# Turning the normed rows of 13 feed-forward blocks with VectorE's 32 x 32 squares and two DMAs, one round ahead, instead of with TensorE's transposes

## The chip, the core and the metric

The kernel runs on one core of a Trainium2 chip. The metric is the device time of one execution in microseconds (us). TensorE (PE) multiplies matrices and writes to PSUM; VectorE (DVE), ScalarE (ACT) and GpSimd (POOL) work element by element; SyncE (SP) only issues DMAs here. PEld is TensorE's weight load. Each engine takes its own instructions strictly in order and waits, where it must, on semaphores of the others.

## What is computed

`x` has 2 x 2048 rows of 256 numbers in float32. Four layers are added to it in turn, each working on layer-normed rows (mean taken off, divided by the standard deviation):

```python
x = x + attn_a(layernorm(x))   # gated scan along the rows of a sequence
x = x + ffn(layernorm(x))      # first feed-forward layer
x = x + attn_b(layernorm(x))   # linear attention, 16 heads, recurrent over the rows
x = x + ffn(layernorm(x))      # second feed-forward layer, same weights
# ffn(y) = gelu(y @ ternary(W1).T + b1) @ ternary(W2).T + b2,  256 -> 1024 -> 256
# ternary(W): each weight is rounded to -1, 0 or 1 by the mean size of W
```

TensorE sums over the partition axis, so the normed rows, which lie with rows on partitions, must be turned (features on partitions) before `y @ W1`. This turning is what the change touches.

## The kernel before

The 4096 rows lie in SBUF as `x_sb`, 32 chunks of 128 rows. Four chunks make a block of 512 rows, so there are 8 blocks (`blocks`, the two sequences in turn). The order of PE, DVE, ACT and POOL instructions is written out by hand (`manual_schedule`); only SP's DMAs are put in order by the framework.

**One feed-forward round** takes one block. `ffn_in` (L491) has 8 steps, one for each 128 hidden features: four matmuls of 512 columns into one PSUM bank (L498; the rows come as two parts, `xh`, the value rounded to fp32r, and `xl`, the rest), then ACT's gelu (L504); after each second step `Hidden.split` calls `halves` (L201): ACT rounds 1024 numbers to `hh` (L203) and DVE subtracts to get `hl` (L204). `ffn_out` (L509) has 8 steps of 8 matmuls (L520); step f needs `hh` and `hl` number f // 2. At its end DVE adds the result to `x_sb` (L529) and, in the second layer, SP stores it (L531).

**Turning.** `norm_stats` (L156) takes four pairs of DVE instructions (L163, L164) and then a chain of small POOL instructions that makes scale and bias of the rows, `rs` and `nb`: L175 (add), L176 (power), L180, L181. `norm_rows` (L184) writes the normed rows `xn` with four ACT instructions (L195). `turned_halves` (L209) turns them: 8 TensorE transposes of 128 x 128 (L216) into two PSUM banks `pt`, and for each bank `halves`: ACT writes `xh` from PSUM (L203), DVE writes `xl` (L204). `ffn_bias` (L534) adds b2 to the next block's rows of `x_sb` with one long POOL instruction (L537). The next round's first matmuls need `xh` and `xl`.

**Another way to turn is already in the kernel.** `norm_squares` (L277): DVE transposes every 32 x 32 square of the rows (L260, `sq`), SP writes them to DRAM (L263, `dsqxn`), SP reads them back with four DMAs that put the squares in their places (L271, `rawxn`, which must wait for the first DMA to land), and `halves_end` (L302) makes `xh` and `xl` out of that in one ACT and one DVE instruction that read with a stride. The attention turns its own rows so, and so is block 1 of the second layer turned (`second_squares`, `second_turned`).

**The front** (L546) holds the scan layer and the first feed-forward layer. After a prologue it runs 8 rounds, i = 0 to 7. Rounds 0 to 3 also carry a unit of the scan: its matmuls (L389, by `scan_steps`) stand between the first four steps of `ffn_in`, and its way back into rows (`a_`, transposes L426, DVE adds L428) and, in rounds 0 to 2, the turning of the next unit's rows (`t_`, TensorE transposes L240, ACT L244 with gamma) stand between steps of `ffn_out`. In rounds 0 to 3 the stats of block i + 2 are taken after `ffn_out` (`fs_`) and the rows of block i + 1 between steps of `ffn_in` (`fr_`). Rounds 4 to 6 also hold `weights_kv` (L463), four POOL instructions of 128 x 512 each. In round 0 to 6, `ft_(i + 1)` turns the next block in the midst of `ffn_out`.

**The attention** follows (not touched), and then the second feed-forward layer, the loop at L1270, called ffn2 below: 8 rounds, of which the first only ends block 0 (its steps, `last.outs`, began within the attention), and rounds 1 to 6 turn block i + 1 on TensorE.

The PSUM banks are given out in rings: six banks ("ps") for everything but the results of `ffn_out`, which have two ("out"). A bank is used again when the ring comes round to it, so TensorE waits if its reader is late.

Of the kernel before, what the change touches and what calls it, by code (L numbers as in the profile page):

```python
# [44 lines left out]
def kernel(  # L45
# [272 lines left out]
    def ternary_sum(pool, w, name, on_vector):  # L318
        wf = w.rearrange("p c e -> p (c e)")
        n = wf.shape[1] // D  # L320
        part = pool.tile([P, n], FP, tag="part", name=f"part_{name}")
        if on_vector:
            nc.vector.tensor_reduce(
                part, wf.rearrange("p (a e) -> p a e", e=D), AX.X, ALU.add, apply_absolute_value=True
            )
            return part
        for k in range(n):
            size = pool.tile([P, D], FP, tag="abs", name=f"abs_{name}{k}")
            nc.scalar.activation(size, wf[:, k * D : (k + 1) * D], AF.Abs, accum_out=part[:, k : k + 1])
        return part  # L330

# [207 lines left out]
    def run(steps, n=None):  # L539
        for _ in steps if n is None else zip(range(n), steps):  # L540
            pass
# [4 lines left out]
    def front(scan_pool, ffn_pool, tern_pool, then, later):  # L546
        last = [{} for _ in range(B)]
        units = [(blocks[0], 2), (blocks[0] + 2, 2)] + [(g0, BC) for g0 in blocks[1:]]
        st, xn, xnT, ys, fst, fn = {}, {}, {}, {}, {}, {}

        def s_(u, bias=True, between=None):
            g0, n = units[u]
            st[u] = norm_stats(scan_pool, chunks(g0, n), rms=True, bias=bias, between=between)

        def r_(u):
            xn[u] = norm_rows(scan_pool, chunks(*units[u]), st.pop(u))

        def t_(u):
            xnT[u] = norm_turned(scan_pool, chunks(*units[u]), xn.pop(u), rms=True)

        def q_(u, e, between=None):
            g0, n = units[u]
            ys.setdefault(u, []).append(scan_part(scan_pool, g0, n, xnT[u], e, last[g0 // CPB], between))

        def a_(u):
            scan_add(*units[u], ys.pop(u))

        def fs_(i, between=None):
            fst[i] = norm_stats(ffn_pool, chunks(blocks[i]), bias=True, between=between)

        def fr_(i):
            fn[i] = norm_rows(ffn_pool, chunks(blocks[i]), fst.pop(i), bufs=1)

        def ft_(i):
            fn[i] = turned_halves(chunks(blocks[i]), fn[i], rows_room(ffn_pool, blocks[i], bufs=1))

        def tern(w, scale, part, **kw):
            nm, to = ("w1", w1r) if w is w1 else ("w2", w2r)
            return ternary_part(tern_pool, w, to, scale, part, nm, **kw)

        scales = {}

        def quarters_1():
            scales[1] = ternary_scale(tern_pool, w1, tot1, "w1")
            tern(w1, scales[1], 0)
            tern(w1, scales[1], 1)

        def quarters_2():
            scales[2] = ternary_scale(tern_pool, w2, tot2, "w2")
            tern(w2, scales[2], 0)  # L590

        s_(0, bias=False)
        r_(0)
        s_(1, bias=False)
        r_(1)
        t_(0)
        s_(2)
        q_(0, 0)
        t_(1)
        q_(0, 1)  # L600
        tot1 = ternary_total(tern_pool, ternary_sum(tern_pool, w1, "w1", True), "w1")
        r_(2)
        q_(1, 0)
        s_(3)
        a_(0)
# [24 lines left out]
        rest_of = tern(w2, scales[2], 2, later=True)  # L630
        ft_(0)
        r_(5)
        q_(4, 1)
        rest_of()
        tern(w2, scales[2], 3)
        nonlocal wo, wv
        wv = const.tile([P, ND, H * DK], FP, tag="wv", name="wv")
        nc.sync.dma_start(out=wv, in_=w_v.rearrange("(c p) e -> p c e", p=P))
        t_(5)
        two_rings()  # L640

        NB = len(blocks)
        for i in range(NB):
            u, g0 = i + 5, blocks[i]
            more, scans = i + 1 < NB, u < len(units)
            hid, staged = hidden(ffn_pool, g0)
            steps = ffn_in(g0, fn.pop(i), hid, staged)
            if i == 0:
                ffn_bias(g0)
            if scans:  # L650
                ys[u] = []
                products = scan_steps(scan_pool, units[u][0], xnT[u], last[units[u][0] // CPB], ys[u])
                for j in range(4):
                    run(products, 1)
                    run(steps, 1)
                    if i == 0 and j == 0:
                        a_(4)
                run(products)
            else:
                run(steps, 4)  # L660
            if u + 1 < len(units):
                s_(u + 1)
            if i == NB - 2:
                then[0]()
            elif scans:
                fr_(i + 1)
            elif i + 2 < NB:
                fs_(i + 2)
            run(steps)
            if not scans and more:  # L670
                fr_(i + 1)
            if u + 1 < len(units):
                r_(u + 1)
            if i == NB - 2:
                then[1]()
            elif not more:
                wo = const.tile([P, NPR, D], FP, tag="wo", name="wo")
                nc.sync.dma_start(out=wo, in_=w_o.rearrange("(c p) e -> p c e", p=P))
                then[2]()

            steps = ffn_out(g0, hid, tag="out")
            if i > 3 and i - 4 < len(later):
                later[i - 4]()
            if i == 2:
                ffn_weights_away()
            if scans:
                run(steps, 2)
                a_(u)
                run(steps, 1)
                ft_(i + 1)  # L690
                run(steps, 2)
                if u + 1 < len(units):
                    t_(u + 1)
                fs_(i + 2)
            else:
                run(steps, 6)
                if more:
                    ft_(i + 1)
            run(steps)
            if more:  # L700
                ffn_bias(blocks[i + 1])
# [554 lines left out]
    with tc.tile_pool(name="keep", bufs=3) as keep_pool:  # L1256
        with (
            tc.tile_pool(name="attn", bufs=1) as attn_pool,
            tc.tile_pool(name="state", bufs=1) as state_pool,
            tc.manual_schedule(engines=by_hand),  # L1260
        ):
            last = Last(keep_pool, attn_pool)
            attention(keep_pool, attn_pool, state_pool, last)

        with tc.tile_pool(name="ffn2", bufs=1) as ffn_pool, tc.manual_schedule(engines=by_hand):
            two_rings()
            steps, rhs = last.outs, last.rhs2
            for i, g0 in enumerate(blocks):  # L1270
                more, more2 = i + 1 < len(blocks), i + 2 < len(blocks)
                if i > 0:
                    hid, staged = hidden(ffn_pool, g0)
                    steps = ffn_in(g0, rhs, hid, staged)
                    run(steps, 4)
                if more2:
                    g2 = blocks[i + 2]
                    st = norm_stats(ffn_pool, chunks(g2), bias=True)
                run(steps)
                if more and i > 0:  # L1280
                    xn = norm_rows(ffn_pool, chunks(blocks[i + 1]), before)
                before = st
                if i > 0:
                    steps = ffn_out(g0, hid, True, "out")
                    run(steps, 6)
                    if more:
                        rhs = turned_halves(chunks(blocks[i + 1]), xn, rows_room(ffn_pool, blocks[i + 1]))
                    run(steps)
                if more:
                    ffn_bias(blocks[i + 1])  # L1290

# [36 lines left out]
```

## Time and profile before

| what | value |
|---|---|
| three runs | 1067.88, 1068.85, 1071.53 us; median 1068.85 |
| the profiled execution: its time, its span, granted TensorE clock | 1071.46 us, 1069.6 us, 0.998 |
| one round of ffn2, from one first matmul of `ffn_in` to the next | 15.93 us |
| one round of the front with a scan unit (rounds 1 to 2, by the sigmoid of the next unit) | 27.93 us |
| one round of the front without (rounds 4 to 6, first matmul to first matmul) | 15.82 us |

The profile is one execution of its own: its time is 2.6 us above the median of the runs, and its span is the stretch from its first to its last instruction. The page gives busy time of each engine; a group of instructions gives line, engine, output and input, count, busy time and mean duration. A timeline gives start, duration, engine, line, operation, and in square brackets how long the engine had been idle before and what ended it. The chain lists, in order of time, the work whose end released the next piece, so that what stands in it sets the end.

### The profile page before, as it was taken

The numbers are of one execution on the slowest core, as the hardware profiler recorded it, in microseconds if no ns is written. First come the engines' busy times: TensorE is split into PE (matmuls) and PEld (weight loads), VectorE is DVE, ScalarE is ACT, GpSimd is POOL, SyncE is SP. The second block draws the span as 40 slices with busy tenths as digits, with TensorE's granted clock in tenths as the row PEclk, the third lists the DMA queues.
The fourth block names the chain that finished last, engine by engine and source line by source line (L and its number), as shares of the span: only waits on it lengthen the run. The fifth ranks groups of instructions, "written<-read, shape, count | busy, mean of one in ns | idle before, by whom it ended". The sixth has DMA issues, their size and how long they took to land. (4 is left out here: it accounts for less than half of the span.)

```text
span 1069.6 us, 43536 instructions
## 1 busy us (share of the span) xinstructions
PE 1055.2 (99%) x20024; PEld 817.7 (76%) x20024; DVE 681.1 (64%) x1041; ACT 596.2 (56%) x826; POOL 171.8 (16%) x290
## 2 busy tenths in 40 slices
PE   9999999999999999999999999999999999999998
PEld 7567779986777777777777777777777777789987
DVE  7975646646675765666666667576665666545654
ACT  4457666855645555445555554555544555447875
POOL 3442224631101001011010010110101111013220
PEclk9999999999999999999999999999999999999999
DMA  9320000003442432424324334233242443111011
GB/s 325 104 79 1 1 1 1 1 21 120 141 134 76 134 113 91 141 74 148 122 66 137 106 117 134 77 133 122 82 141 90 133 130 102 52 60 41 20 40 40
DMA packets 71463, 97.58 MB, mean 91 GB/s; under 512 B 7280, under 2 KB 58864, under 8 KB 71024
## 3 DMA queue, kind: packets, MB, share of 16 engines
q1 hardware_dynamic: 69664, 92.43, 26.2%
q8 instruction: 157, 2.57, 1.0%
q10 hardware_dynamic: 1584, 2.36, 0.9%
q14 instruction: 26, 0.21, 0.1%
q0 software_dynamic: 32, 0.00, 0.0%
HBM read 50.99 MB, written 43.78 MB: 89 GB/s over the span
## 5 line engine op out<-in xcount | busy, mean ns | idle before, releaser
L841 DVE TENSOR_TENSOR p<-hp,mask 128x512 f32<-128x512 f32 x128 | 82.1, 682 | 85.1 <-PE hp L835 85.1
L915 PE MATMUL hy<-wo,oT 128*128 128x256 f32 x512 | 124.0, 386 | 1.2 <-PE hqT_X L776 0.7
L204 DVE TENSOR_TENSOR hl<-h,hh 128x1024 fp32r<-128x1024 f32 x60 | 74.0, 1237 | 64.7 <-ACT hh L203 64.6
L915 PEld LDWEIGHTS hy<-wo,oT 128*128 128x128 f32 x512 | 93.6, 190 | 20.7 <-issue 7.3
L504 ACT ACTIVATE h<-h,b_sb 128x512 f32<-128x512 f32 x120 | 77.7, 682 | 50.3 <-PE h L498 50.2
L733 POOL TENSOR_TENSOR S<-xnT 128x128 f32<-128x128 f32 x30 | 13.8, 460 | 515.4 <-ACT xnT L313 515.4
L877 ACT COPY uT<-huT 128x512 f32<-128x512 f32 x32 | 18.7, 585 | 129.1 <-PE huT L866 129.1
L195 ACT ACTIVATE xn<-x_sb,nb,rs 128x256 f32<-128x256 f32 x124 | 65.1, 591 | 17.1 <-POOL nb L181 17.1
L904 DVE TENSOR_TENSOR S<-S,hS 128x512 f32<-128x512 f32 x60 | 41.2, 687 | 42.0 <-PE hS L892 39.0
L934 ACT COPY kT<-rawkT 128x1024 f32<-128x1024 f32 x32 | 66.7, 2084 | 0.0
L260 DVE STREAM_TRANSPOSE sqkT<-kN 128x1024 f32<-128x1024 f32 x32 | 65.8, 2055 | 1.3 <-ACT kN L812 1.2
L260 DVE STREAM_TRANSPOSE squN<-uT 128x1024 f32<-128x1024 f32 x31 | 63.6, 2052 | 4.0 <-ACT uT L879 3.6
L934 ACT COPY uN<-rawuN 128x1024 f32<-128x1024 f32 x31 | 64.7, 2086 | 1.2 <-DMA rawuN<-dsquN 0.9
L203 ACT CAST hh<-h 128x1024 fp32r<-128x1024 f32 x60 | 63.0, 1050 | 1.9
L520 PE MATMUL o<-w2r,hh 128*128 128x256 f32 x256 | 62.1, 284 | 0.0
L520 PE MATMUL o<-w2r_back,hh 128*128 128x256 f32 x248 | 60.3, 284 | 0.9 <-DVE x_sb L529 0.9
L520 PE MATMUL o<-w2r,hl 128*128 128x256 f32 x256 | 60.9, 279 | 0.0
L520 PE MATMUL o<-w2r_back,hl 128*128 128x256 f32 x248 | 59.9, 282 | 0.0
L498 PE MATMUL h<-xh,w1r 128*128 128x512 f32 x128 | 58.6, 458 | 0.0
L812 ACT COPY vN<-hvN_X 128x512 f32<-128x512 f32 x16 | 9.4, 586 | 78.8 <-PE hvN_X L781 78.8
L163 DVE BATCH_NORM_STATS2 st<-x_sb 128x6 f32<-128x256 f32 x128 | 51.4, 402 | 2.4 <-DMA x_sb<-in_x_dram 2.4
L892 PEld LDWEIGHTS hS<-kN 64*64 64x64 f32 x1984 | 32.8, 135 | 23.2 <-issue 22.4
(221 smaller groups left out, 2477.1 us busy)
## 6 DMA issues: line engine op xcount, KB each, us to landing
dsqkT<-sqkT SPq DMA_DIRECT2D x32, 512.0 KB, 3.8
rawkT<-dsqkT SPq DMA_DIRECT2D x128, 128.0 KB, 3.0
dsquN<-squN SPq DMA_DIRECT2D x31, 512.0 KB, 3.3
rawuN<-dsquN SPq DMA_DIRECT2D x124, 128.0 KB, 3.0
out_dram<-x_sb SPq DMA_DIRECT2D x15, 256.0 KB, 2.3
x_sb<-in_x_dram SPq DMA_DIRECT2D x7, 512.0 KB, 8.9
dsqxn<-sqxn SPq DMA_DIRECT2D x14, 256.0 KB, 3.8
rawxn<-dsqxn SPq DMA_DIRECT2D x56, 64.0 KB, 2.6
```

The source lines that it names most:

```text
L163: nc.vector.bn_stats(st[:, c, :], x_sb[:, g, :])
L195: nc.scalar.activation(xn[:, c, :], x_sb[:, g, :], AF.Identity, bias=nb[:, c : c + 1], scale=rs[:, c : c + 1],)
L203: copy(hi, src)
L204: nc.vector.tensor_tensor(lo, src, hi, ALU.subtract)
L260: nc.vector.transpose(to, src)
L498: nc.tensor.matmul(ph, lhsT=w1r[:, d, f * P : (f + 1) * P], rhs=r[:, d, :], start=(d == 0 and k == 0), stop=(d == ND - 1 and k == 1),)
L504: nc.scalar.activation(h[:, f % 2, :], ph, AF.Gelu, bias=b1_sb[:, f : f + 1])
L520: nc.tensor.matmul(to, lhsT=h[f // 2][:, f % 2, c * P : (c + 1) * P], rhs=w2r[:, f, :], start=(f == 0 and k == 0 and c % 2 == 0), stop=(f ...
L841: nc.vector.tensor_tensor(d[s][nm][:, h], banks[h], mask8, ALU.mult)
L904: nc.vector.tensor_tensor(t, prev, banks[c], ALU.add)
L915: nc.tensor.matmul(py, lhsT=d[s]["oT"][:, p, :], rhs=wo[:, p, :], start=(p == 0), stop=(p == NPR - 1),)
L934: act(t, d[s]["r" + nm].rearrange("p t q -> p q t"))
```

## The change

13 blocks are turned by squares and two DMAs instead of by TensorE: blocks 1 to 7 in the front and blocks 2 to 7 in ffn2. Block 0 of the front and of ffn2 keep their transposes. Where a round i did the rows of block i + 1 and turned them at once, it now does three things: it takes the stats of block i + 2 within `ffn_in`; after the first step of `ffn_out` it ends block i + 1 (`halves_end`, from squares that were sent off in the round before); and right behind that it makes the rows of block i + 2, their squares and issues their DMAs. The order on ACT at that place becomes: last `hh`, (rows of the next scan unit,) `xh`, four row instructions L195, (L244 of the next unit). The order on DVE becomes: last `hl`, `xl`, squares L260, (L428,) L529. The rows of block 1 in the front are made and sent off within round 0, behind the first step of `ffn_in` and `a_(4)`. The buffer `abs` of the weight preparation goes from two to one.

```diff
+        def fq_(i):
+            fr_(i)
+            fn[i] = norm_squares(ffn_pool, chunks(blocks[i]), [fn[i]], 1)
+
+        def fe_(i):
+            fn[i] = halves_end(fn[i], rows_room(ffn_pool, blocks[i], bufs=1))
...
                     if i == 0 and j == 0:
                         a_(4)
+                        fq_(1)
...
-            if i == NB - 2:
+            if i + 2 < NB:
+                fs_(i + 2)
+            elif more:
                 then[0]()
-            elif scans:
-                fr_(i + 1)
-            elif i + 2 < NB:
-                fs_(i + 2)
             run(steps)
-            if not scans and more:
-                fr_(i + 1)
...
+            run(steps, 1)
+            if more:
+                fe_(i + 1)
+            if i + 2 < NB:
+                fq_(i + 2)
+            elif more:
+                then[1]()
             if scans:
-                run(steps, 2)
+                run(steps, 1)
                 a_(u)
-                run(steps, 1)
-                ft_(i + 1)
-                run(steps, 2)
+                run(steps, 3)
                 if u + 1 < len(units):
                     t_(u + 1)
-                fs_(i + 2)
-            else:
-                run(steps, 6)
-                if more:
-                    ft_(i + 1)
             run(steps)
...
 # ffn2
                 if more2:
-                    g2 = blocks[i + 2]
-                    st = norm_stats(ffn_pool, chunks(g2), bias=True)
+                    cs = chunks(blocks[i + 2])
+                    st = norm_stats(ffn_pool, cs, bias=True)
+                if i > 0:
+                    run(steps)
+                    steps = ffn_out(g0, hid, True, "out")
+                run(steps, 1)
+                if more and i > 0:
+                    rhs = halves_end(raw, rows_room(ffn_pool, blocks[i + 1]))
+                if more2:
+                    raw = norm_squares(ffn_pool, cs, [norm_rows(ffn_pool, cs, st)], 1)
                 run(steps)
-                if more and i > 0:
-                    xn = norm_rows(ffn_pool, chunks(blocks[i + 1]), before)
-                before = st
-                if i > 0:
-                    steps = ffn_out(g0, hid, True, "out")
-                    run(steps, 6)
-                    if more:
-                        rhs = turned_halves(chunks(blocks[i + 1]), xn, rows_room(ffn_pool, blocks[i + 1]))
-                    run(steps)
```

More of the change, by code (lines that the diff above doesn't have):

```diff
@@ L327, in ternary_sum @@
         for k in range(n):
-            size = pool.tile([P, D], FP, tag="abs", name=f"abs_{name}{k}")
+            size = pool.tile([P, D], FP, tag="abs", bufs=1, name=f"abs_{name}{k}")
             nc.scalar.activation(size, wf[:, k * D : (k + 1) * D], AF.Abs, accum_out=part[:, k : k + 1])
@@ L662, in front @@
                 s_(u + 1)
-            if i == NB - 2:
+            if i + 2 < NB:
+                fs_(i + 2)
+            elif more:
                 then[0]()
-            elif scans:
-                fr_(i + 1)
-            elif i + 2 < NB:
-                fs_(i + 2)
             run(steps)
-            if not scans and more:
-                fr_(i + 1)
             if u + 1 < len(units):
                 r_(u + 1)
-            if i == NB - 2:
-                then[1]()
-            elif not more:
+            if not more:
                 wo = const.tile([P, NPR, D], FP, tag="wo", name="wo")
```

## The prediction

> **What bounds the kernel now.** I read the page's busy times first, then the chain, then the groups by shape, then the timelines of POOL, DVE and ACT in the stages that change.
>
> ```profile
> PE 1055.2 (99%) x20024; PEld 817.7 (76%) x20024; DVE 681.1 (64%) x1041; ACT 596.2 (56%) x826; POOL 171.8 (16%) x290
> ```
> ```profile
> 986.22 7.46 PE h L498 x32
> 993.67 5.70 PE o L520 x48
> 999.38 0.87 PE pt L216 x8
> 1000.25 1.90 PE o L520 x16
> ```
>
> The chain (start, duration, what) has nothing but TensorE in ffn2, and one round's 8 transposes stand in it whole with 0.87 us. The front's rounds are as full: 27.92 us there against 12 + 32 + 64 matmuls and 24 transposes, without gaps over 0.3 us. TensorE bounds both stages; the question is only which other engine becomes late when each round is 0.87 us shorter. The prices of the new way stand in the trace:
>
> ```profile
> L204 DVE TENSOR_TENSOR xl<-rawxn,xh 128x1024 fp32r<-128x1024 f32 x1 | 2.1, 2054 | 4.6 <-ACT xh L203 4.6
> L203 ACT CAST xh<-rawxn 128x1024 fp32r<-128x1024 f32 x1 | 2.0, 2047 | 0.0
> L260 DVE STREAM_TRANSPOSE squN<-uT 128x1024 f32<-128x1024 f32 x31 | 63.6, 2052 | 4.0 <-ACT uT L879 3.6
> ```
> ```profile
> 935.43 0.34 SPq L263 DMA_DIRECT2D dsqxn<-sqxn  x1
> 939.39 2.66 SPq L271 DMA_DIRECT2D rawxn<-dsqxn  x4
> ```
>
> Squares and both strided halves take 2.05 us each. The DMAs: the second can't be issued before the first has landed, 3.96 us after; four issues take 1.7 to 2.7 us and the last lands 2.8 us later. From squares to rows in place: 7.6 us at best, 9.1 us here; I take 8.4. And this couples POOL with DVE:
>
> ```profile
> 104.74 1.22 DVE L204 TENSOR_TENSOR hl<-h,hh 128x1024 fp32r<-128x1024 f32 x1
> ```
> ```profile
> 104.90 1.95 POOL L176 TENSOR_TENSOR rs<-rs,mhalf 128x4 f32<-128x4 f32 x1 [5.57 <-DVE rs L173]
> ```
> ```profile
> 187.41 2.41 POOL L537 TENSOR_TENSOR x_sb<-x_sb,b_sb 128x1024 f32<-128x1024 f32 x1
> ```
> ```profile
> 188.69 3.47 DVE L204 TENSOR_TENSOR hl<-h,hh 128x1024 fp32r<-128x1024 f32 x2 [2.78 <-ACT hh L203]
> ```
>
> The power L176 takes 1.04 us elsewhere; begun inside an `hl` it ended 0.89 us after the `hl` did. Two `hl`s, 2.45 us elsewhere, took 3.47 when L537 was under way. So a DVE subtraction with both inputs in SBUF and a POOL instruction wait for each other, whoever began first. Beside the old `xl`, whose input is in PSUM, L537 ran in its usual 2.41 us. The new `xl` reads SBUF alone: I count it among those that collide, for 2.05 us.
>
> **The change, part by part.** Removed on TensorE: 13 x 0.87 = **11.3 us**. (13 blocks x 8 are 104 of the 120 transposes of L216; the built program has just these fewer, so that the change takes place is no question.) Per block ACT pays 2.05 for 2 x 0.59, DVE 2.05 + 2.05 for 2 x 0.68, SP five more DMAs. None of that is on the path by itself: an ffn2 round becomes 15.06 us, and ACT's sum in it is 13.3, DVE's 12.5. What decides is the order.
>
> *Scan rounds 0 to 2 of the front.* TensorE's t_ needs `xn` of the scan; its stats end as now, 18.63 us into the round, and POOL's chain, now beside L163 (one input) and no longer beside `hl`, is done at 20.34 in place of 22.2. No row shows whether L163 holds POOL; between nothing and one L163 (0.4 us) each time I take nothing, as its second input is missing, and t_ has 0.9 us of room. So t_, at 23.35, doesn't wait (done 22.46). Then: ffn stats end at 20.75, `hl` 2 and 3 hold POOL till 23.1, L176 ends 0.89 later, L181 starts at 24.39; `xl` starts at 24.43, 0.04 later, so L181 gets through. Rows of block i + 2 on ACT end at 26.7, then L244 to 27.3, and the next round's first matmul, due at 27.05, starts at 27.35. Gain 0.57 each, **1.7**.
>
> *Round 3* has no t_ and no L244. L537 now starts before `xl` and holds it 2 us, which ends at 26.05, when TensorE is due. Gain **0.9**.
>
> *Rounds 4 to 7.* Round 4: rows landed (squares end 2.0 us into the round, + 8.4 = 10.4), `xh` from 10.5, `xl` 12.6 to 14.65, due 15.0: gain 0.9. But L180 reaches POOL at 12.8, behind `xl`'s start, and waits to its end; so the four L463 instructions (5.1 us) and L537 start 2 us later than they would and run into round 5. There L537 is under way from 5.2 to 7.6 us when `hl` 0 is due at 5.5. ffn_out needs that at 7.5: it gets it at 8.7, and `hl` 2 after the stats 0.65 late. Loss 1.9 against 0.9 saved: -1.0. Round 6 the same way -1.2, round 7 -0.3. Together **-1.6**. If `hl` 0 wins against L537, `hl` 1 is behind it and the price is the same; if it met none of them, this part would be +3.5.
>
> *ffn2 round 1.* Rows of block 2 were made a round later; now they stand on ACT at 955.3 in front of the first gelu (955.35 now), 2 us. Squares end at 959.45, rows land at 967.9, `xh` and `xl` to 972.0; the next round starts now at 970.3. **-1.5** (-0.7 with 7.6 us of DMA, -2.2 with 9.1).
>
> *ffn2 rounds 2 to 6.* If the gelus start on time (1.1 us into the round), the last `hh` is done at 10.5, `xh` and `xl` follow to 14.65: no stall, + 0.87. L180, at 12.8, falls at the start of `xl` (12.6 to 12.8, by when rows land). Behind it, the rows and so the next gelus and squares come 1.1 us late, the DMAs land at 12.2 to 12.8 and that round takes 15.6 to 16.7, in which POOL is through in time again. So rounds can alternate, with a mean of 15.3 to 15.9; I take 15.4, since with DMAs of 8.4 us or more `xl` starts late enough for POOL in most rounds. Against 15.93 now: 5 x 0.5 = **2.5** (0 to 4.4).
>
> Sum: 1.7 + 0.9 - 1.6 - 1.5 + 2.5 = **2.0 us off**: 1071.46 - 2.0 = 1069.5 for the profiled execution, whose time is 2.6 above the median of 1068.85. On the median: **1067**.
>
> Hidden at no cost: dsqxn of block 1 goes out at 67.9 behind two 1 MB DMAs issued at 64 that take 8.4 us; its rows are due at 80.6, 4 us after they land. `xl` of the other rounds is before L529, which delays nothing until the "out" banks are used, 3 us later. L428 frees its banks 1 us before TensorE's next use. The stores of ffn2 stand on SP between the two DMAs, which the first DMA's landing covers. `abs` with one buffer: all on ACT, in order.
>
> [...] In the trace a short one in flight held nothing: L176 at 195.58 for 1.04 us, `hl` from 195.63 in its usual 1.22. [...]
>
> **Rivals.**
> - *All hidden.* POOL slips in before `xl`, DMAs land in 7.6 us, L463 meets no `hl`. 11.3 less 3 x 0.3: 10.4 off, **1058.5**. For it: 36% idle DVE, 44% idle ACT. Against: L180's place behind two `hl`s, which is the same in every round.
> - *Slower: L181 behind `xl` in the scan rounds.* By my sum it wins by 0.04 us. If it loses, the rows wait to the end of `xl`, ACT reaches L244 2.2 us later and TensorE stands for xnT in rounds 0 to 2: 3 x 2.2 = 6.6 on top of 1067, **1073.5**.
> - *Slower by the DMA's way.* At 473.0 the second DMA was issued 4.9 us after the first; with that, 10 us in all. 1.6 us later in the eight rounds where `xh` waits for rows (ffn2 1 to 6, front 5 and 6), some of it in slack: about 8, **1075**.
>
> **How the numbers follow.** Forecast 0.38, all hidden 0.24, L181 late 0.22, DMA late 0.16. What a measurement can tell from no change is 0.3%, 3.2 us. The forecast has +-4 of its own (1063 to 1071), a third of it beyond 3.2 us: faster 0.24 + 0.12 = 0.36; slower: nearly all of the last two with a tail of the forecast, 0.33; same 0.31. The range reaches from all hidden to the DMA case with its bound of 9.6 (8 + 1.6): 1058 to 1077.
>
> **What would show it.** In the new profile: L216 x16 in place of x120; L180 and L181 with 1 to 2 us in place of 0.2 in ffn2, and idle PE before h (L498) on `xl`; PE waiting for xnT L244 in the front if L181 lost; `hl` over 2 us in rounds 5 to 7; ACT's `xh` waiting for DMA rawxn in ffn2. I am wrong if the strided `xl` does not block POOL, or if stalls sit in the attention, where nothing should change.

## Result and the profile after

The changed kernel is **slower by 0.7%**: 1078.42 us (median of 6 runs, 1074.18 to 1079.91) against 1069.88 (1067.88 to 1071.80) of the kernel before on the same chip, ratio 1.0071 [1.0048, 1.0093]. The profiled execution took 1078.41 us with a span of 1076.6.

The page's busy times and the groups by shape of the changed kernel:

```profile
PE 1050.0 (98%) x19920; PEld 807.6 (75%) x19920; DVE 732.3 (68%) x1041; ACT 612.8 (57%) x813; POOL 189.5 (18%) x290
```
```profile
L204 DVE TENSOR_TENSOR hl<-h,hh 128x1024 fp32r<-128x1024 f32 x60 | 78.4, 1318 | 30.7 <-ACT hh L203 30.7
...
L204 DVE TENSOR_TENSOR xl<-rawxn,xh 128x1024 fp32r<-128x1024 f32 x14 | 40.5, 2894 | 20.8 <-ACT xh L203 20.8
```

104 transposes are gone (x20024 to x19920), but TensorE's busy time fell by 5.2 us only; a stretch at half clock, shown below, counts as busy (2.10 of 2.10 us at a granted clock of 0.52, from 1010.50) and is part of the difference. (The fastest kernel below, with the same matmuls, has 1044.1, or 11.1 less.) POOL has the same 290 instructions and is busy 17.7 us longer: the time that they wait for DVE counts as theirs (L175 of 128x4 has a mean of 893 ns for 352, L180 of 522 for 362, and two of L468 took 2.9 us for 1.3). `xl`, 2054 ns when it met nobody, has a mean of 2894.

Where the time went, from the starts of rounds on TensorE (first matmul to first matmul, us; ffn2 from the first matmul of its round 1 to the end of the last matmul). A wait at the start of a round counts to that round, also where it is the rows of the round before that were late:

| stretch | before | after | difference | predicted |
|---|---|---|---|---|
| prologue and scan round 0 | 86.19 | 85.58 | -0.6 | -0.6 |
| scan rounds 1, 2 | 27.93, 27.93 | 27.89, 27.88 | -0.1 | -1.1 |
| round 3 | 26.95 | 26.74 | -0.2 | -0.9 |
| rounds 4, 5, 6, 7 | 15.83, 15.81, 15.82, 14.94 | 14.93, 17.00, 16.20, 16.48 | +2.2 | +1.6 |
| attention, to ffn2's round 1 | 722.83 | 725.00 | +2.2 | 0 |
| ffn2 rounds 1 to 6 | 15.89, 15.93, 15.94, 15.93, 15.93, 15.94 | 16.00, 17.14, 15.34, 18.71, 15.06, 16.91 | +3.6 | -1.0 |
| last round | 16.53 | 16.54 | 0 | 0 |

The attention's code is unchanged, and in the twelve profiles of this study it took 719.9 to 725.0 us; in e7 below, with the same front ahead of it, 721.9. Its 2.2 us are left to chance.

**A scan round.** Timeline of the changed kernel in round 1, from where L181 gets through:

```profile
110.49 0.23 POOL L181 TENSOR_SCALAR nb<-nb 128x4 f32<-128x4 f32 x1
110.69 2.40 POOL L537 TENSOR_TENSOR x_sb<-x_sb,b_sb 128x1024 f32<-128x1024 f32 x1
110.76 2.08 ACT L195 ACTIVATE xn<-x_sb,nb,rs 128x256 f32<-128x256 f32 x4
110.78 4.14 DVE L204 TENSOR_TENSOR xl<-rawxn,xh 128x1024 fp32r<-128x1024 f32 x1 [1.54 <-ACT xh L203]
...
114.84 2.01 DVE L260 STREAM_TRANSPOSE sqxn<-xn 128x1024 f32<-128x1024 f32 x1
...
116.71 1.26 DVE L428 TENSOR_TENSOR x_sb<-x_sb,py 128x512 f32<-128x512 f32 x2
...
117.43 0.50 PE L498 MATMUL h<-xh,w1r 128*128 128x512 f32 x1 [0.26 <-DVE x_sb L428]
```

L181 won, as the sum had it. But what stands right behind it on POOL is L537, and it began 0.09 us before `xl`, which then took 4.14 us: until L537 was done, and its own 2 us besides. Squares and L428 follow 2 us late, and the first `ffn_in` matmul of the next round (L498) needs the bank that L428 frees: it comes 3.96 us after the round's first matmul at 113.47. In the kernel before it came after 3.03:

```profile
114.12 3.59 PE L389 MATMUL pq<-xnT,wqkva 128*128 128x512 f32 x8
117.15 0.79 PE L498 MATMUL h<-xh,w1r 128*128 128x512 f32 x1
```

The 0.9 us saved in a round are given back there, at the start of the next one; so rounds 1, 2 and 3 show the loss and round 0 does not.

**A pair of ffn2 rounds.** The rounds alternate. Timelines of the changed kernel at the end of round 2 and of round 3:

```profile
988.67 2.21 DVE L204 TENSOR_TENSOR xl<-rawxn,xh 128x1024 fp32r<-128x1024 f32 x1 [0.97 <-ACT xh L203]
988.67 2.22 POOL L180 TENSOR_TENSOR nb<-mv,rs 128x4 f32<-128x4 f32 x1
...
991.25 1.59 ACT L195 ACTIVATE xn<-x_sb,nb,rs 128x256 f32<-128x256 f32 x3 [2.61 <-POOL nb L181]
```
```profile
1003.61 2.29 ACT L203 CAST xh<-rawxn 128x1024 fp32r<-128x1024 f32 x1 [1.06 <-DMA rawxn<-dsqxn]
1003.66 0.22 POOL L180 TENSOR_TENSOR nb<-mv,rs 128x4 f32<-128x4 f32 x1
...
1004.16 2.40 POOL L537 TENSOR_TENSOR x_sb<-x_sb,b_sb 128x1024 f32<-128x1024 f32 x1
...
1005.93 2.43 DVE L204 TENSOR_TENSOR xl<-rawxn,xh 128x1024 fp32r<-128x1024 f32 x1 [2.11 <-ACT xh L203]
...
1008.42 0.50 PE L498 MATMUL h<-xl,w1r_back 128*128 128x512 f32 x1 [1.84 <-DVE xl L204]
```

In round 2, L180 (0.2 us of work) began together with `xl` and ended with it; the rows on ACT begin 2.6 us after `xh` (the view ends before the fourth of them), and with them the next round's gelus, squares and DMAs are late. In round 3 POOL is through in time, but the rows of the round before land 1.06 us late, L537 still overlaps `xl`, and TensorE waits 1.84 us. After that wait came a second cost. Windows of the changed kernel (stretch, length, then busy time and, in brackets, count for PE, PEld, DVE, ACT, POOL; then the granted clock):

```profile
1006.20:1008.40 2.20, 0.37 (x3) 0.06 (x1) 2.20 (x2) 1.68 (x4) 0.37 (x1) 1.00 0.00 0
1008.40:1010.50 2.10, 2.08 (x6) 1.68 (x7) 2.10 (x2) 0.69 (x1) 0.00 (x0) 0.67 0.00 0
1010.50:1012.60 2.10, 2.10 (x6) 1.62 (x5) 0.98 (x2) 1.32 (x2) 0.00 (x0) 0.52 0.65 259
1012.60:1016.00 3.40, 3.40 (x16) 2.72 (x15) 1.66 (x2) 3.20 (x5) 0.00 (x0) 1.00 0.90 253
```

TensorE was granted half its clock for 3.4 us, by these windows; seven matmuls stand 0.42 to 0.43 us apart there in place of 0.23, and one at either end 0.31 to 0.34, 1.5 us more in all. With the wait ahead of it, this is why round 4 took 18.71.

### The profile page after: what moved, and what is told of

The parts are those of the page before. It is cut to its first block, busy times and chain, and to the rows that moved or that the text cites. A ratio compares the mean times of both kernels' runs of the same rounds, so it can differ in the third digit from the quotient of the medians.

```text
span 1076.6 us, 43496 instructions
## 1 busy us (share of the span) xinstructions
PE 1050.0 (98%) x19920; PEld 807.6 (75%) x19920; DVE 732.3 (68%) x1041; ACT 612.8 (57%) x813; POOL 189.5 (18%) x290
## 3 DMA queue, kind: packets, MB, share of 16 engines
q10 hardware_dynamic: 1584, 2.36, 0.9%
## 4 chain that ended last, share of the span: by engine, by line
PE 83%; DVE 6%; ACT 5%; issue 3%; POOL 2%; DMA 1%; SPq 0%; ACTq 0%; DVEq 0%; POOLq 0%
PE hy L917 11%; PE h L498 6%; PE hkN_X L783 6%; PE hp L837 6%; PE hqT_X L778 6%; PE hvN_X L783 5%; PE o L520 5%; PE pq L369 4%; PE hoT L854 3%; PE huT L854 3%; PE huT L868 3%; PE hS L894 3%; PE hoT L868 3%; PE pq L389 3%; PE hqT_Z L778 3%
## 5 line engine op out<-in xcount | busy, mean ns | idle before, releaser
L204 DVE TENSOR_TENSOR hl<-h,hh 128x1024 fp32r<-128x1024 f32 x60 | 78.4, 1318 | 30.7 <-ACT hh L203 30.7
L879 ACT COPY uT<-huT 128x512 f32<-128x512 f32 x32 | 18.7, 585 | 128.9 <-PE huT L868 128.9
L195 ACT ACTIVATE xn<-x_sb,nb,rs 128x256 f32<-128x256 f32 x124 | 65.3, 592 | 26.6 <-POOL nb L181 26.6
L260 DVE STREAM_TRANSPOSE sqkT<-kN 128x1024 f32<-128x1024 f32 x32 | 65.8, 2057 | 1.3 <-ACT kN L814 1.2
L260 DVE STREAM_TRANSPOSE squN<-uT 128x1024 f32<-128x1024 f32 x31 | 63.6, 2052 | 4.0 <-ACT uT L881 3.6
L498 PE MATMUL h<-xh,w1r 128*128 128x512 f32 x128 | 57.8, 451 | 0.8 <-DVE x_sb L428 0.8
L260 DVE STREAM_TRANSPOSE sqxn<-xn 128x512 f32<-128x512 f32 (+1 forms) x29 | 46.6, 1613 | 13.6 <-ACT xn L195 13.6
L175 POOL TENSOR_SCALAR rs<-mv 128x2 f32<-128x2 f32 (+1 forms) x34 | 17.8, 524 | 211.4 <-DVE mv L164 211.1
L204 DVE TENSOR_TENSOR xl<-rawxn,xh 128x1024 fp32r<-128x1024 f32 x14 | 40.5, 2894 | 20.8 <-ACT xh L203 20.8
```

The costliest lines, as they stand in the source:

```text
L195: nc.scalar.activation(xn[:, c, :], x_sb[:, g, :], AF.Identity, bias=nb[:, c : c + 1], scale=rs[:, c : c + 1],)
L204: nc.vector.tensor_tensor(lo, src, hi, ALU.subtract)
L260: nc.vector.transpose(to, src)
L498: nc.tensor.matmul(ph, lhsT=w1r[:, d, f * P : (f + 1) * P], rhs=r[:, d, :], start=(d == 0 and k == 0), stop=(d == ND - 1 and k == 1),)
```

## Experiments

Three theories. **A**: POOL and DVE stand in each other's way, so that small POOL instructions end late, and `xl` and `hl` with them. **B**: the DMAs' way of 7 to 8 us sets the rounds. **C**: the work added on ACT and DVE does. The table gives time and ratio, then from the profiles the rounds, the begin of the attention and ffn2's length; the rows of "before" and "after" are those of above. The expectations of e1 to e4 count ffn2 to the end of the span, 3.1 to 3.4 us more than the last column: 115.4 before, 118.9 after, 115.2 in e1, 117.7 in e2, 116.9 in e3 and 115.5 in e4.

| kernel | median, us | ratio to before | scan rounds 1, 2 | rounds 4 to 7 | attention begins | ffn2 rounds 1 to 6 | ffn2 |
|---|---|---|---|---|---|---|---|
| before | | 1 | 27.93, 27.93 | 15.83, 15.81, 15.82, 14.94 | 231.4 | 15.9 each | 112.1 |
| after | 1078.42 | 1.0071 [1.0048, 1.0093] | 27.89, 27.88 | 14.93, 17.00, 16.20, 16.48 | 232.7 | 16.00, 17.14, 15.34, 18.71, 15.06, 16.91 | 115.7 |
| e1_front_only | 1071.58 | 1.0022 [1.0009, 1.0035] | 27.90, 27.96 | 14.93, 17.07, 16.24, 16.49 | 232.8 | 15.9 each | 112.1 |
| e2_ffn2_only | 1073.42 | 1.0036 [1.0020, 1.0051] | 27.93, 27.95 | 15.84, 15.81, 15.82, 14.94 | 231.4 | 16.01, 17.21, 15.24, 15.84, 17.11, 15.07 | 114.3 |
| e3_stats_early | 1072.40 | 1.0026 [1.0010, 1.0041] | 29.20, 28.64 | 14.92, 15.27, 15.54, 15.41 | 230.7 | 19.04, 15.68, 15.74, 15.72, 15.74, 15.20 | 113.7 |
| e4_bias_early | 1070.05 | 1.0005 [0.9993, 1.0016] | 27.45, 27.38 | 14.93, 17.13, 16.21, 16.43 | 231.3 | 16.08, 16.28, 15.21, 16.72, 15.17, 16.23 | 112.2 |
| e5_mixed | 1066.70 | 0.9969 [0.9956, 0.9983] | 27.37, 27.36 | 14.93, 15.22, 15.69, 15.32 | 227.5 | 16.05, 16.23, 15.60, 15.61, 15.64, 15.58 | 111.3 |
| e7_no_dma_wait | 1075.24 | 1.0057 [1.0037, 1.0077] | 27.97, 27.90 | 14.94, 17.01, 16.22, 16.50 | 232.8 | 15.86, 17.18, 15.11, 18.71, 14.97, 16.96 | 115.3 |
| e8_nb_dve_only | 1088.96 | 1.0178 [1.0152, 1.0204] | 30.83, 30.89 | 14.93, 16.38, 16.00, 16.51 | 240.7 | 17.88, 16.89, 16.99, 16.99, 16.99, 16.90 | 119.2 |
| e9_nb_on_dve | 1068.71 | 0.9984 [0.9972, 0.9997] | 27.30, 27.25 | 14.93, 16.36, 15.97, 16.44 | 229.8 | 18.75, 15.38, 15.15, 15.14, 15.14, 15.16 | 111.3 |
| e10_nb_dve_kv | 1064.59 | 0.9950 [0.9934, 0.9966] | 27.25, 27.24 | 14.93, 15.13, 15.14, 14.94 | 226.4 | 17.86, 15.92, 15.17, 15.14, 15.06, 15.31 | 111.0 |
| e11_round0_pool | 1062.89 | 0.9942 [0.9926, 0.9959] | 27.31, 27.25 | 14.93, 15.14, 15.15, 14.94 | 226.2 | 16.01, 16.25, 15.11, 15.22, 15.31, 15.06 | 109.5 |

**The two halves of the change: e1_front_only and e2_ffn2_only.** In the first the loop of ffn2, in the second the front is that of the kernel before.

> The change in the front alone; ffn2 turns on TensorE as before. Theory A (POOL and DVE in each other's way: L180 behind xl, L537 ahead of it, and what follows from late rows) and its rivals B (the DMAs' way of 7 to 8 us) and C (the added work on ACT and DVE itself) expect the same here: the front ends 1.3 us later than before, as in the profile of the change (first matmul of the attention at 232.7 for 231.4), ffn2 as before (115.4 us from its round 1 to the end), together 1071. If the 2.2 us that the attention was longer belong to the change (banks or places in SBUF given out differently), they show here too: 1073.5. If they are chance, not.

> The change in ffn2 alone; the front turns on TensorE as before. All theories: the front ends at 231.4, ffn2 takes 118.9 us for 115.4 and alternates between rounds of about 15.2 and 17.5 us; together 1073.5. With e1 it tells whether the parts add up.

Each half alone costs something, 1.9 and 3.8 us over the 1069.65 of the kernel before beside them: together 5.7 of the 8.5. The front of e1 has the rounds of the whole change to 0.1 us, and the first three rounds of ffn2 in e2 have them too. From the fourth on they part: e2 has no half-clock stretch in ffn2 and takes 114.3 us there, 1.4 less than the changed kernel. The attention took 723.5 and 719.9 us, so e1's question is answered on the side of chance.

**POOL's chain earlier: e3_stats_early.** The stats of block i + 2 are taken at the start of round i (from round 1 on), so that L180 and L181 are done before `xl`:

```diff
+            if i > 0 and i + 2 < NB:
+                fs_(i + 2)
             if scans:
                 ys[u] = []
...
 # ffn2
+                if more2:
+                    cs = chunks(blocks[i + 2])
+                    st = norm_stats(ffn_pool, cs, bias=True)
                 if i > 0:
                     hid, staged = hidden(ffn_pool, g0)
                     steps = ffn_in(g0, rhs, hid, staged)
                     run(steps, 4)
-                if more2:
-                    cs = chunks(blocks[i + 2])
-                    st = norm_stats(ffn_pool, cs, bias=True)
```

> The change, with the stats of block i + 2 taken at the start of round i, ahead of the round's hl, in the front from round 1 on and in ffn2. POOL's chain to nb is then done by about 10 us into an ffn2 round, before xl can stand in its way at 12.6. A: rows follow xh at once, gelus start on time in each round, ffn2 rounds 2 to 6 are 15.1 to 15.5, ffn2 110 to 113 us in all. B: rows land late as before, rounds 16 and more, 116 us or more. C: ACT and DVE have the same to do, 118. In the front scan rounds stay as they are with L537 ahead of xl (A).

The alternation of ffn2 is gone in rounds 2 to 5, as A has it, and the front's rounds 5 to 7 fall by 3.5 us together. But the rounds are at 15.68 to 15.74 in place of A's 15.1 to 15.5, and ffn2 as a whole, 116.9 us in the expectation's count, is where B had it and not at A's 110 to 113. The four stats now stand on DVE ahead of the first `hl`. Timeline of this kernel in round 1 of ffn2, where rows stand ahead of the gelus as well:

```profile
962.06 2.33 DVE L204 TENSOR_TENSOR hl<-h,hh 128x1024 fp32r<-128x1024 f32 x2
...
963.31 0.39 PE L520 MATMUL o<-w2r_back,hl 128*128 128x256 f32 x1 [2.23 <-DVE hl L204]
963.35 1.27 ACT L504 ACTIVATE h<-h,b_sb 128x512 f32<-128x512 f32 x2 [2.41 <-DVE hl L204]
...
965.86 3.35 POOL L537 TENSOR_TENSOR x_sb<-x_sb,b_sb 128x1024 f32<-128x1024 f32 x1
...
967.97 2.32 DVE L204 TENSOR_TENSOR hl<-h,hh 128x1024 fp32r<-128x1024 f32 x1 [1.02 <-ACT hh L203]
```

TensorE waits for `hl` 2.23 us, the gelu 2.41 (`h` has two buffers). And L537, which follows L181, now meets the last `hl` in place of `xl`: 2.32 us for 1.23. Round 1 lost 3 us and the scan rounds 1.3 and 0.8, so on the whole little was won: an order that frees one instruction moved the collision to another.

**L537 moved: e4_bias_early.** L537 of block i + 2 stands right behind that block's rows, and so runs beside the squares:

```diff
             if i + 2 < NB:
                 fq_(i + 2)
+                ffn_bias(blocks[i + 2])
...
-            if more:
-                ffn_bias(blocks[i + 1])
```

> The change, with the bias L537 of a block issued right behind its squares, a round before: POOL does it at the start of a round, when DVE has no subtraction of two SBUF inputs. A: in the scan rounds xl takes 2.05 us for 4.14, TensorE no longer waits for L428, and a round is 27.2 to 27.4 us for 27.9; rounds 5 to 7 lose less by up to 1 us each; ffn2 keeps its alternation, since L180 is behind xl as before (118). B and C: no change anywhere.

Timeline of this kernel in round 1, to be held against the one above:

```profile
109.94 0.24 POOL L181 TENSOR_SCALAR nb<-nb 128x4 f32<-128x4 f32 x1
110.22 2.09 ACT L195 ACTIVATE xn<-x_sb,nb,rs 128x256 f32<-128x256 f32 x4
110.22 2.32 DVE L204 TENSOR_TENSOR xl<-rawxn,xh 128x1024 fp32r<-128x1024 f32 x1 [1.54 <-ACT xh L203]
112.20 1.25 ACT L244 ACTIVATE xnT<-pt,gam 128x512 f32<-128x512 f32 x2
112.39 2.37 POOL L537 TENSOR_TENSOR x_sb<-x_sb,b_sb 128x1024 f32<-128x1024 f32 x1 [2.21 <-ACT xn L195]
112.45 2.08 DVE L260 STREAM_TRANSPOSE sqxn<-xn 128x1024 f32<-128x1024 f32 x1
```

`xl` takes 2.32 for 4.14, the squares meet L537 without loss, and each scan round takes 0.5 us less than in the changed kernel (27.45, 27.38, round 3 26.27). Rounds 5 to 7, where `weights_kv` (L463) collides, stay, and so does the alternation of ffn2 by L180. Its late rounds are shorter than expected, though, 16.2 to 16.7 in place of 16.9 to 18.7, and ffn2 takes 112.2 in place of 115.7: `xl` met L537 in them too. What is left of them is a wait of TensorE of up to 1.4 us for an `xl` behind rows that landed late, since L180 had held them up. One POOL instruction at another place takes 8.4 us off 1078.42 in the medians; 4.9 of that stand in the front and ffn2 of the profiles, the rest is with the attention, where chance has its share.

**Both, where each had helped: e5_mixed.** L537 as in e4; stats early in rounds 4 and 5 of the front and 2 to 5 of ffn2 only.

> L537 stands right behind the block's squares, and the stats of block i + 2 stand at the start of the round in rounds 4 and 5 of the front and 2 to 5 of ffn2 (where this alone had left L180 free), but at their old place in the scan rounds and in round 1 of ffn2 (where it had cost 1.3 and 3 us). Theory A (POOL and DVE in each other's way): no rows wait for POOL there, rounds 3 to 6 of ffn2 take 15.1 to 15.3 us, and ffn2 from its first matmul of round 1 to the end 109.5 to 110.5 us in place of 115.7 (changed kernel) and 112.1 (before); the attention begins at 228 to 229 us in place of 232.7; time 3 to 6 us under the kernel before. Theory B (the DMAs' way of 7 to 8 us sets the rounds): xh waits for DMA as often as now, ffn2 112 us or more, time within 2 us of the kernel before. Theory C (the added work of ACT and DVE sets the round): ffn2 rounds at 15.7 or more whatever stands where.

Time (2.6 us under the kernel before) and front (227.5) fall near what A wants. ffn2 does not: 111.3 us, with rounds of 15.6 in place of 15.1 to 15.3. Rows wait neither for POOL nor for DMA there; the first `hl` begins 1.6 us after its `hh` (988.76 against 987.15), behind the four stats, and the last `hh` is late with it. This half microsecond is theory C's, by way of the order on DVE.

**No wait for the DMAs: e7_no_dma_wait.** The halves of ffn2 read a fixed tile:

```diff
+            still = ffn_pool.tile([P, P, BC * ND], FP, tag="still", name="still")
+            nc.gpsimd.memset(still, 0.5)
...
-                    rhs = halves_end(raw, rows_room(ffn_pool, blocks[i + 1]))
+                    rhs = halves_end(still, rows_room(ffn_pool, blocks[i + 1]))
```

> The changed kernel, but in ffn2 the halves of blocks 2 to 7 are taken from a fixed tile that POOL fills once with 0.5, so that no engine waits for the DMAs; squares and DMAs still run. It leaves out the turned rows in ffn2. Theory B: without the DMAs' landing all rounds of ffn2 are alike, 15.06 to 15.2 us, and ffn2 takes 108 to 109.5 us in place of 115.7. Theory A: L180 is still held by xl, the gelus of the next round are still late; rounds of 16 to 17 us remain and ffn2 takes 111 us or more, up to the 115.7 of now. Theory C: every round 15.9 or more, 113 to 115.7 us.

Timeline of this kernel, the same place as round 3 above:

```profile
999.08 2.27 ACT L203 CAST xh<-still 128x1024 fp32r<-128x1024 f32 x1
...
1000.80 2.40 POOL L537 TENSOR_TENSOR x_sb<-x_sb,b_sb 128x1024 f32<-128x1024 f32 x1
...
1001.39 3.59 DVE L204 TENSOR_TENSOR xl<-still,xh 128x1024 fp32r<-128x1024 f32 x1 [0.93 <-ACT xh L203]
...
1005.04 0.50 PE L498 MATMUL h<-xl,w1r_back 128*128 128x512 f32 x1 [1.82 <-DVE xl L204]
```

Nothing is won: 115.3 us, the same rounds to 0.25 us, and TensorE's wait is 1.82 for 1.84. `xh` no longer waits, `xl` starts earlier, meets L537 earlier and takes 3.59 us. The wait for the DMAs in the changed kernel lay beside the collision, and taking it away alone wins nothing: B falls as the cause. C's 15.9 or more in every round does not show either: rounds 3 and 5 take 15.11 and 14.97.

**Less work on POOL: e8_nb_dve_only.** L180 and L181 become one DVE instruction of 128x4 ahead of `xl`; L537 stays where the change has it. (In this and the next kernels L169 and L170 are the first two of POOL's chain, and L181 is the new instruction on DVE.)

```diff
+    def norm_bias(pool, cs, stats):
+        mv, rs, _ = stats
+        nb = pool.tile([P, BC], FP, tag="nb", name=f"nb{cs[0]}")
+        nc.vector.scalar_tensor_tensor(nb, mv[:, :, 0], -1.0, rs, ALU.mult, ALU.mult)
+        return mv, rs, nb
...
 # ffn2 (the front likewise)
                 run(steps, 1)
+                if more2:
+                    st = norm_bias(ffn_pool, cs, st)
                 if more and i > 0:
                     rhs = halves_end(raw, rows_room(ffn_pool, blocks[i + 1]))
```

> The changed kernel, with the bias of the rows (L180 and L181) as one small DVE instruction between the last hl and xl, and L537 left at its old place, so that on POOL it now follows the power L176 at once. POOL has less to do and no row waits for L180. Theory A: L537 starts before that small DVE instruction or before xl and holds it for up to 2.4 us in every round of ffn2 (in the kernel with L537 moved the small one took 2.36 us in place of 0.15 in the one place where L537 came first); rounds 2 to 6 at 16.5 to 17.4 us, ffn2 116 to 120 us; scan rounds 28 us or more; time 1078 to 1086 us, no better than the changed kernel. Theory B or C: nothing is gained or lost by L537; the time is that of the changed kernel or less, 1074 to 1078 us.

Timeline of this kernel at the end of a round of ffn2:

```profile
994.00 1.97 POOL L170 TENSOR_TENSOR rs<-rs,mhalf 128x4 f32<-128x4 f32 x1
995.95 2.39 POOL L537 TENSOR_TENSOR x_sb<-x_sb,b_sb 128x1024 f32<-128x1024 f32 x1
996.00 2.36 DVE L181 SCALAR_TENSOR_TENSOR nb<-mv,rs 128x4 f32<-128x4 f32 x1 [0.93 <-POOL rs L170]
998.28 2.01 DVE L204 TENSOR_TENSOR xl<-rawxn,xh 128x1024 fp32r<-128x1024 f32 x1
...
1000.35 0.50 PE L498 MATMUL h<-xl,w1r_back 128*128 128x512 f32 x1 [1.66 <-DVE xl L204]
```

The kernel with the least work on POOL is the slowest of all, 1.8% over the kernel before, since L537 now comes right behind the power, 0.05 us ahead of a DVE instruction of four numbers a partition, which it holds for 2.36 us. Rounds 2 to 6 of ffn2 have 16.9 to 17.0 us, inside the 16.5 to 17.4 that A gave. The time is 3 us above A's range. Something that A didn't have stands in the scan rounds: TensorE waits 1.92 us for `xnT`, and its clock is then granted at 0.50 for some 3 us (88 to 91, likewise in the next two).

**L537 moved as well: e9_nb_on_dve.** e8 with e4's place for L537.

> L537 stands right behind the block's squares, and the bias of the rows (L180 and L181) is one small DVE instruction between the last hl and xl, so that POOL has nothing to do between the power and the rows. The stats stay where the change put them. Theory A: rows follow xh on ACT at once in every round; ffn2 rounds 2 to 6 take 15.06 to 15.3 us, ffn2 108 to 109.5 us in place of 115.7; scan rounds 27.1 to 27.4; rounds 5 and 6 of the front stay at 16 to 17 us, since L463 still collides with xl and hl there; time 3 to 6 us under the kernel before. Theory B: rows are in time but the DMAs aren't; TensorE waits for xl behind xh behind DMA rawxn, ffn2 112 us or more. Theory C: ffn2 at 112 us or more with ACT or DVE busy without a break ahead of xl.

Timeline of this kernel, first between rounds 0 and 1 of ffn2, then at the end of round 2:

```profile
952.61 2.40 POOL L537 TENSOR_TENSOR x_sb<-x_sb,b_sb 128x1024 f32<-128x1024 f32 x1
952.67 2.36 DVE L181 SCALAR_TENSOR_TENSOR nb<-mv,rs 128x4 f32<-128x4 f32 x1 [1.62 <-POOL rs L170]
```
```profile
984.04 0.16 DVE L181 SCALAR_TENSOR_TENSOR nb<-mv,rs 128x4 f32<-128x4 f32 x1 [0.93 <-POOL rs L170]
984.24 2.08 ACT L195 ACTIVATE xn<-x_sb,nb,rs 128x256 f32<-128x256 f32 x4 [0.27 <-DVE nb L181]
984.31 2.20 DVE L204 TENSOR_TENSOR xl<-rawxn,xh 128x1024 fp32r<-128x1024 f32 x1
```

20 us less than e8 in the median, by the place of L537 alone: the small instruction takes 0.16 us, rows follow at once, and rounds 2 to 6 are steady at 15.14 to 15.38, most of them 0.1 above the 15.06 that TensorE needs. The added work and the DMAs are all there, so neither C nor B sets these rounds. Round 1 lost 2.8 us at the one place where L537 (of block 1) still came first, which puts ffn2 at 111.3 and not at A's 108 to 109.5, and rounds 5 to 7 of the front still lose to `weights_kv`; so the gain is 0.2% only, less than A's 3 to 6 us.

**L463 moved: e10_nb_dve_kv.** `weights_kv` at the starts of rounds 1 to 3:

```diff
-            if i > 3 and i - 4 < len(later):
-                later[i - 4]()
...
+            if 0 < i <= len(later):
+                later[i - 1]()
             if scans:
                 ys[u] = []
```

> As the kernel with the bias of the rows on DVE, and L463 (weights_kv) moved from rounds 4 to 6 of the front to the starts of rounds 1 to 3. Theory A: ffn2 as there (108 to 109.5 us); rounds 4 to 7 of the front take 14.95 to 15.2 us each, the scan rounds at most 0.5 us more than there; the attention begins at 226.5 to 228 us in place of 232.7 (231.4 in the kernel before), the time is 6 to 10 us under the kernel before. Theory B: rounds 4 to 7 still wait for rows (xh behind DMA rawxn), 15.8 us or more; time not under the kernel before by more than 3 us. Theory C: the same, without a wait for DMA.

Rounds 5 to 7 take 14.94 to 15.14 us in place of e9's 15.97 to 16.44, and the attention begins 5.0 us earlier than in the kernel before, as A had it. The whole gain, 4.7 us, is under A's 6 to 10: ffn2 is at 111.0, by round 1 again.

**The last collision: e11_round0_pool.** In round 0 of ffn2 the bias stays on POOL, ahead of L537:

```diff
-                    st = norm_stats(ffn_pool, cs)
+                    st = norm_stats(ffn_pool, cs, bias=(i == 0))
...
-                if more2:
+                if more2 and i > 0:
                     st = norm_bias(ffn_pool, cs, st)
```

> As the kernel with the bias on DVE and L463 moved, but in round 0 of ffn2 the bias stays on POOL, ahead of L537, since the small DVE instruction was held by L537 for 2.3 us there and round 1 took 17.9 us. Theory A: round 1 takes 16.0 us and waits for xl fall with it, ffn2 108 to 109.5 us in place of 111.0, the front as there (attention begins at 226 to 227 us); time 6 to 9 us under the kernel before, 2 us under that kernel. Theories B and C: round 1 stays at 17 us or more, since rows still stand ahead of its gelus; ffn2 111 us.

Round 1 takes 16.01 us, ffn2 109.5 (109.51, the upper end of A's range), the time is 5.9 us under the kernel before, at the edge of the 6 to 9 expected. This is the fastest kernel of the study, **faster than both**: 0.9942 [0.9926, 0.9959]. Of the 11.3 us removed from TensorE, the stages of its profile show 5.2 us in the front and 2.6 in ffn2. What is not won in ffn2 is round 1 (rows ahead of its gelus: 0.95 over the 15.06, and then 0.93 us of waiting for `xl`) and up to 0.25 in rounds 3 to 6.

## Why the prediction was wrong, step by step

The forecast was 1067 us and 2.0 off; the runs show 8.5 on, and 1078.42 lies above the range of 1058 to 1077 as well. In the profiles the span grew by 7.0: 1.3 in the front, 2.2 in the attention (chance), 3.6 in ffn2. (The profiled execution of the kernel before is itself 1.6 us above the median beside the changed kernel.) Of the 9.0 us between forecast and profile, 4.1 are in rounds 2 to 6 of ffn2, 1.7 in rounds 0 to 3 of the front, 0.6 in its rounds 4 to 7, 0.5 in round 1 of ffn2 and 2.2 in the attention. The mechanism named was the right one, and A is shown by e4, e8, e9 and e10; its bookkeeping was not carried through. Two things failed: L537, which follows the small instructions on POOL, was not followed into `xl` in scan rounds 0 to 2 and in ffn2; and the alternating rounds of ffn2 were valued near the lower end of their mean.

- **Scan rounds 0 to 2: failed.** "L181 gets through" held, by more than the 0.04 us given. The step stopped there. L537, the next on POOL, holds `xl`; for round 3 the text had counted just this, for the rounds before it hadn't. "L428 frees its banks 1 us before TensorE's next use", under what is hidden, falls with it: L428 came 2 us late, and TensorE lost 0.9 at the start of rounds 1, 2 and 3. -2.6 was forecast for rounds 0 to 3 and -0.9 came (0.6 of it by round 0). e4 shows it: L537 moved, 0.5 more in each. What was said of round 3 itself, that its held `xl` ends when TensorE is due, fits: round 4 behind it took 14.93.
- **Rounds 4 to 7: the mechanism was right, the sum near (+2.2 for +1.6), its parts less so.** Round 4 gained its 0.9. In round 5, L537 starts late behind `weights_kv` and holds the first two `hl`, as the text had it:

```profile
188.37 2.40 POOL L537 TENSOR_TENSOR x_sb<-x_sb,b_sb 128x1024 f32<-128x1024 f32 x1
188.78 4.21 DVE L204 TENSOR_TENSOR hl<-h,hh 128x1024 fp32r<-128x1024 f32 x2
```

  Rounds 5, 6 and 7 lost 1.2, 0.4 and 1.5 for 1.0, 1.2 and 0.3. With TensorE's waits for `xl` at the start of rounds 6 and 7 (0.95 and 1.22 us) put to the round whose rows were late, it is 2.1, 0.7 and 0.3: round 5 cost double, round 6 half. e10 shows the cause: with `weights_kv` out of the way, all four are at 15.14 or less.
- **ffn2 round 1: the number near, in part by luck.** -1.5 was forecast (its own times, 972.0 against a start at 970.3, make 1.7). 2.0 came: 0.1 in the round and 1.89 us of TensorE's wait for `xl` right behind its end. That rows ahead of the first gelu make the round late was right. But the DMAs took 1.0 us less than assumed, which alone would have made the loss smaller, and L537 made `xl` 1.0 us longer than its 2.05, which the text hadn't counted:

```profile
971.74 2.41 POOL L537 TENSOR_TENSOR x_sb<-x_sb,b_sb 128x1024 f32<-128x1024 f32 x1
972.93 3.01 DVE L204 TENSOR_TENSOR xl<-rawxn,xh 128x1024 fp32r<-128x1024 f32 x1 [1.53 <-ACT xh L203]
```

- **ffn2 rounds 2 to 6: failed; the term was mis-sized.** "So rounds can alternate" is what happened, and in the way described. But of its 15.3 to 15.9 the mean of 15.4 was chosen, on the ground that with DMAs of 8.4 us or more `xl` starts late enough for POOL in most rounds. They took 7.2 to 7.9 in ffn2, and in rounds 2 and 4 `xl` started with L180 or 0.05 us ahead of it: L180 lost every second time. With TensorE's waits put to the round whose rows were late, rounds 2 to 6 took 15.25, 17.18, 16.87, 16.64 and 15.33. The late rounds are 16.6 to 17.2 where 15.6 to 16.7 was forecast, since L537 meets `xl` in rounds 3 and 5 too (e4 shows its share) and 1.5 us of round 4 are half clock. Without that clock the mean is 15.9, the upper end of the forecast and, by chance, the old round: what TensorE no longer does is waited for. 2.5 off was forecast, 1.6 on came (3.5, less the 1.89 that belongs to round 1): the late rounds used up all that was saved, and the clock made the rest.
- **DMAs: mis-sized.** 8.4 us from squares to rows was too much. SyncE's timeline of the changed kernel in round 1 of ffn2:

```profile
963.35 0.34 SPq L263 DMA_DIRECT2D dsqxn<-sqxn  x1
963.76 1.23 SPq L531 DMA_DIRECT2D out_dram<-x_sb  x2
966.00 1.77 SPq L271 DMA_DIRECT2D rawxn<-dsqxn  x4
```

  The squares had ended at 963.2, the second DMA went out 2.65 us after the first (3.96 and 4.9 in the rows of before), and `xh` began at 970.60, freed by it: 7.4. Rows that land earlier still win nothing (e7); what the 8.4 did was to carry the choice of 15.4.
- **The rivals.** "L181 behind `xl`" did not occur in the scan rounds; e8 shows what such a loss costs: TensorE waits 1.92 us for `xnT` in each. "The DMA's way" gave a time near the one measured (1075) for a reason that e7 and e9 rule out. Of the 10.4 us of "all hidden", e11 reaches 5.9, by the same way of turning with L537, L463 and the bias of the rows at other places.
- **Not foreseen:** some waits of TensorE are followed by a stretch at half clock, which cost 1.5 us on top of the 1.84 of the wait in round 4 of ffn2.

## What to carry to other kernels

When work moves from TensorE to VectorE, list the DVE instructions that now have both inputs in SBUF (here `xl`, 2.05 us alone and up to 4.16 beside L537), and walk POOL's queue past each of them to its end, the long instruction behind the short ones above all; the cure here was to put the long one beside DVE work that it does not disturb. (Squares begun 0.05 to 0.06 us behind L537 took 2.08 us in e4, at 112.45, and 2.24 in e5, at 983.29; those of the changed kernel that met no L537 took 2.01 to 2.34. In the kernel before, the two adds from PSUM of L529 took 1.29 us beside L537, at 969.92, and 1.28 without it, at 231.20.) A price per instruction says little: here the same instructions made 1089, 1069 or 1065 us (e8, e9, e10) by their order. And a stall that recurs in alternate rounds has to be summed over two rounds, not valued at its better one.

## What the runs showed of the hardware

- **Four numbers a partition can wait for a thousand.** A DVE instruction of 128x4 with two inputs in SBUF took 0.16 us alone and 2.36 beside L537 (e9). The other way round, L180, 0.20 us alone, took 2.22 beside `xl` (988.67 in the changed kernel). But the POOL power begun 0.02 to 0.18 us before an `hl` held nothing, four times in the changed kernel: L176 at 1002.55 for 1.04 us, `hl` at 1002.59 in its 1.24. So the runs show the collision for the long L537 and for POOL behind an `hl` or `xl`; that the short power holds an `hl` begun behind it, no row shows. Why is not shown.
- **Half clock with waits of about 2 us.** In the changed kernel one of three waits of 1.6 to 1.9 us in ffn2 was followed by 3.4 us at a granted clock of 0.5; e7 has it at the same place. The attention's last step has a wait of 2.07 us for `M` (timelines of before, after, e8 and e11); in all twelve profiles the windows around it have 2.07 to 2.30 us without a matmul. In seven of them, the kernel before among them, half clock began between 0.7 us before the end of the wait and 1.3 us behind it. Windows of the kernel before right behind that wait, which ends at 906.8:

```profile
906.00:908.00 2.00, 1.22 (x71) 1.22 (x75) 1.90 (x4) 0.84 (x2) 0.00 (x0) 0.93 0.50 129
908.00:910.00 2.00, 2.00 (x65) 1.88 (x59) 1.73 (x2) 0.00 (x0) 0.00 (x0) 0.50 0.03 11
910.00:912.00 2.00, 2.00 (x8) 1.59 (x8) 1.06 (x2) 0.45 (x1) 0.00 (x0) 0.72 0.64 262
```

  So the same wait has it in some executions and not in others. It goes with 1.6 to 2.6 us more: from the end of that wait to TensorE's next one, for `uN`, are 15.9, 16.5 and 15.9 us in before, after and e8, which have it, and 14.3, 13.9 and 13.9 in e2, e3 and e11, which don't. What decides is not shown. Every other half-clock stretch between the prologue and the last matmul came with a wait too: 1.84 us in the changed kernel, 1.82 in e7, 1.9 in each of three scan rounds of e8, 2.23 in e3, and in e9 1.50 us without a matmul from 960 to 962. Of the attention's 2.2 us, 0.6 lie in this stretch, at half clock in both kernels.
